# ScalarE's instruction order written out by the program, with the exponentials of masked scores one step behind those taken straight from PSUM

## The chip, the cores and the metric

The kernel runs on one core of one Trainium2 chip. Its time is the device time of one execution, in microseconds (us). The kernel before takes 4256.9 us (the median of 3 executions, 4254.99 to 4259.61). The profile below is of one more execution, with a span of 4253.7 us. TensorE's granted clock was 0.98 of full speed in it.

In what follows PE is TensorE (its matmuls), PEld TensorE's weight loads, ACT ScalarE, DVE VectorE, POOL GpSimd and SP the engine that issues most DMAs. SBUF is the on-chip memory for operands, PSUM the one into which TensorE writes.

## What is computed

Four layers of a graph network run over x, 16 sequences of 1024 nodes with 128 features, with one 1024 x 1024 adjacency matrix for all of them. Three layers are attention layers of 8 heads (16 features a head), each followed by an output projection, a layer norm, a feed-forward part of width 256 and a second layer norm. The fourth is a graph attention layer whose scores are sums of two node values. Cut to what matters here, an attention layer is:

```python
scores = jnp.einsum('bnhd,bmhd->bhnm', Q, K) / jnp.sqrt(16.)
scores = jnp.where(mask, -jnp.inf, scores)          # mask: adj == 0
attn = jax.nn.softmax(scores, axis=-1)
attn_out = jnp.einsum('bhnm,bmhd->bnhd', attn, V).reshape(B, N, OUT_DIM)
x = layer_norm(x + attn_out @ Wo + bo)
x = layer_norm(x + relu(x @ W1 + b1) @ W2 + b2)
```

## The kernel before

**Blocks and steps.** A block is one sequence b in one attention layer l. There are 48 of them, in an order that takes four sequences through three layers side by side. A block has 32 steps: 2 groups g of four heads, 2 halves qh of 512 queries, 8 tiles kt of 128 keys. So there are 1536 steps, numbered n in the main loop (from L703).

**What one step does.** `score_step` (L387) takes an SBUF tile e for the four heads and works on two pairs of heads, pp = 0 and 1. For each pair TensorE writes scores for two heads into a PSUM slot of 128 x 1024 (L395). What then turns scores into masked exponentials goes one of two ways:

- pp = 0 with kt in 0, 1, 3, 4, 6: ScalarE takes the exponential straight out of PSUM (L402), and GpSimd multiplies it by a mask of zeros and ones (L403). There are 960 of these. I call the exponential **direct**.
- pp = 1, and pp = 0 too with kt in 2, 5, 7 (`BOTH_ON_DVE`): VectorE adds a mask of 0 and -57344 while it copies the scores out of PSUM (L405), and ScalarE takes the exponential in place in SBUF (L406). There are 2112 of these. I call this exponential **masked**.

A PSUM slot is free again when L402 or L405 has read it. There are three slots (`slot`, L121), and a step takes two. The fourth layer's edge scores (L569, read by L572) take slots of the same three.

**Four steps later** `av_step` (L409) multiplies e by V on TensorE and adds up in one PSUM bank (L412). The delay is `AHEAD = 4`. There are six e tiles. After the eight tiles kt of a half, `finish` (L415) has VectorE transpose the sums (L423) and take reciprocals (L425), and GpSimd scale them (L426, into A).

**Pieces.** All other work (projections, output projection, feed-forward, the fourth layer) is cut into pieces, and a step takes at most one (`piece`, L642), from chains with due times. A piece writes one PSUM bank, of which there is one only (`bank`, L125). So the next piece's matmuls wait until the bank has been copied out, by ScalarE (L263, L265, L359, L366, L468, L533, L534, L548) or VectorE (L303, L360, L537, L587). For Q and K both do: ScalarE copies a rounded part (hi, L359), then VectorE the remainder (lo, L360).

**Who sets the order.** A scheduler in the compiler decides at build time in which order each engine's instructions stand, from priorities and its own idea of durations; the order does not change while the kernel runs. `soon()` (L251) gives the copies out of the pieces' bank a higher priority. The loop stands inside `tc.manual_schedule` (L704) for TensorE: there instructions stay as the program writes them, score, av, piece, step after step. In the kernel before, this holds for TensorE alone. ScalarE, VectorE and GpSimd are ordered by the scheduler. [...]

In this order of ScalarE the masked exponentials of step n stand, as a rule, before the direct one of step n+1.

## Time and profile before

| engine | busy us | share of the span |
| --- | --- | --- |
| PE (matmuls) | 3892.9 | 92% |
| POOL | 3451.4 | 81% |
| ACT | 3417.3 | 80% |
| DVE | 3404.9 | 80% |
| PEld (weight loads) | 1575.2 | 37% |

The columns come from the first part of the profile page. "Busy" is the time in which at least one instruction of the engine was running. Ends of matmuls are modelled, so a busy TensorE is not TensorE at its peak. DMA is small: the queues moved 232.23 MB, 55 GB/s on average.

A row of the groups of instructions reads: line, engine, operation, tile written <- tiles read, shapes, count | busy us, mean ns of one | idle time of the engine just before them, and which instruction ended most of that idle time. A row of the waits reads: who waited <- for whom: us in total, times, longest. A row of the timeline reads: start, duration, engine, line, operation, tiles, count of merged instructions, and in brackets the idle time before it and what ended it. PEld rows wait while earlier matmuls still run, so a wait shown there is only partly lost time; a wait shown at PE is time without a matmul.

### The profile page before, as it was taken

How to read it: one execution, taken by the hardware profiler on the slowest of the kernel's cores; microseconds unless marked ns; L12 is line 12 of the kernel's file. 1: busy time of each engine (PE TensorE's matmuls, PEld its weight loads, DVE VectorE, ACT ScalarE, POOL GpSimd, SP SyncE). 2: the span in 40 equal slices, each digit the busy share in tenths (PEclk: the TensorE clock that was granted, in tenths of full speed). 3: DMA queues.
4: the chain of work that ended last, by engine and by line, in shares of the span. 5: the costliest groups of instructions: out<-in, count | busy, mean ns of one | idle time of the engine just before them, and what ended most of it. 6: DMA issues, size and time to landing. Idle time of an engine off the chain costs nothing.

```text
span 4253.7 us, 93788 instructions
## 1 busy us (share of the span) xinstructions
PE 3892.9 (92%) x37589; PEld 1575.2 (37%) x37589; DVE 3404.9 (80%) x5324; ACT 3417.3 (80%) x3961; POOL 3451.4 (81%) x3010
## 2 busy tenths in 40 slices
PE   7999999999999999999999899999999999999986
PEld 2333333344443333334444333333344433333435
DVE  6888888877777888887777888887877788888784
ACT  7999999876778898987676898997876789998770
POOL 4788888876779888888777988888877798888785
PEclk9999999999999999999999999999999999999997
DMA  5221222121211221221112212221211212212100
GB/s 147 65 61 50 52 61 61 48 63 44 51 51 48 61 61 44 57 61 51 51 44 59 59 48 55 61 61 41 56 48 49 66 41 61 60 47 55 44 24 17
DMA packets 126235, 232.23 MB, mean 55 GB/s; under 512 B 36704, under 2 KB 75616, under 8 KB 125792
## 3 DMA queue, kind: packets, MB, share of 16 engines
q1 hardware_dynamic: 122896, 225.14, 21.0%
q8 instruction: 299, 4.90, 0.5%
q10 hardware_dynamic: 2896, 1.01, 0.1%
q14 instruction: 144, 1.18, 0.1%
HBM read 15.54 MB, written 8.39 MB: 6 GB/s over the span
## 4 chain that ended last, share of the span: by engine, by line
PE 37%; DVE 26%; ACT 23%; issue 7%; POOL 5%; DMA 1%; SPq 1%; DVEq 0%; ACTq 0%; POOLq 0%
DVE e L405 16%; ACT e L406 13%; PE t L271 11%; PE acc L412 10%; PE s L395 9%; ACT e L402 6%; PE t L581 6%; DVE st L296 2%; POOL e L403 2%; DVE tt L423 1%; DVE e L572 1%; DVE x L303 1%; PE t L260 1%; ACT xT L265 1%; DVE lo L360 1%
## 5 line engine op out<-in xcount | busy, mean ns | idle before, releaser
L405 DVE TENSOR_TENSOR e<-s,mask_add 128x1024 f32<-128x1024 f32 x2112 | 2499.4, 1212 | 441.2 <-PE s L395 351.5
L406 ACT ACTIVATE e<-e 128x1024 f32<-128x1024 f32 x2112 | 2200.2, 1060 | 408.2 <-DVE e L405 392.1
L403 POOL TENSOR_TENSOR e<-e,mask 128x1024 f32<-128x1024 f32 x960 | 2054.0, 2151 | 426.1 <-ACT e L402 410.5
L412 PE MATMUL acc<-e,v 128*17 128x512 f32 x12288 | 1635.4, 604 | 56.5 <-DVE tt L423 29.8
L395 PE MATMUL s<-Wq,Wk 64*128 64x512 f32 x6144 | 1225.7, 462 | 137.9 <-ACT e L402 67.9
L402 ACT ACTIVATE e<-s 128x1024 f32<-128x1024 f32 x960 | 980.4, 1021 | 115.0 <-PE s L395 58.4
L395 PEld LDWEIGHTS s<-Wq,Wk 64*128 64x128 f32 x6144 | 505.8, 185 | 1118.5 <-issue 371.5
L412 PEld LDWEIGHTS acc<-e,v 128*17 128x17 f32 x12288 | 207.2, 95 | 558.2 <-issue 445.6
L315 POOL TENSOR_SCALAR x<-x,mv 128x128 f32<-128x128 f32 x896 | 391.4, 452 | 24.1
L319 POOL TENSOR_TENSOR x<-x,ln_g 128x1024 f32<-128x1024 f32 (+1 forms) x97 | 229.4, 2365 | 107.8 <-PE t L260 101.9
L581 PEld LDWEIGHTS t<-hd,e 128*128 128x128 f32 x2048 | 255.2, 205 | 63.7 <-issue 32.5
L581 PE MATMUL t<-hd,e 128*128 128x129 f32 x2048 | 267.2, 292 | 8.3 <-DVE x L587 3.5
L313 POOL TENSOR_TENSOR mv<-mv,half_neg 128x4 f32<-128x4 f32 x224 | 232.4, 1037 | 14.7
L271 PE MATMUL t<-x1T,W 128*32 128x512 f32 x1536 | 206.2, 609 | 18.0 <-ACT hT L468 8.6
L303 DVE TENSOR_TENSOR x<-t,x 128x512 f32<-128x512 f32 x192 | 131.8, 687 | 100.1 <-PE t L271 99.4
L296 DVE BATCH_NORM_STATS2 st<-x 128x6 f32<-128x128 f32 x896 | 196.7, 279 | 2.8
L271 PEld LDWEIGHTS t<-W,hT 128*32 128x32 f32 x6144 | 172.0, 111 | 70.6 <-issue 32.9
L271 PE MATMUL t<-W,hT 128*32 128x128 f32 x6144 | 187.1, 274 | 9.1 <-DVE x L303 5.2
L260 PE MATMUL t<-identf,x 128*128 128x128 f32 x896 | 151.5, 290 | 34.7 <-ACT xT L265 7.8
L260 PEld LDWEIGHTS t<-identf,x 128*128 128x128 f32 x896 | 95.9, 142 | 229.2 <-issue 48.0
L311 POOL TENSOR_SCALAR mv<-mv 128x4 f32<-128x4 f32 x224 | 53.0, 237 | 145.1 <-DVE mv L298 108.4
L468 ACT ACTIVATE hT<-t,b 128x512 f32<-128x512 f32 x192 | 132.3, 689 | 45.6 <-PE t L271 42.6
(83 smaller groups left out, 2509.7 us busy)
## 6 DMA issues: line engine op xcount, KB each, us to landing
Wk<-hi SPq DMA_DIRECT2D x384, 128.0 KB
Wk<-lo SPq DMA_DIRECT2D x384, 128.0 KB
Wq<-hi SPq DMA_DIRECT2D x384, 128.0 KB
Wq<-lo SPq DMA_DIRECT2D x384, 128.0 KB
x<-in_x_dram SPq DMA_DIRECT2D x16, 512.0 KB
out_dram<-x SPq DMA_DIRECT2D x31, 256.0 KB
ai<-in_adj_dram SPq DMA_DIRECT2D x8, 512.0 KB
g_rows<-parts SPq DMA_DIRECT2D x124, 4.0 KB
```

Source lines behind the costliest of these rows:

```text
L260: nc.tensor.transpose(ps[:, t * P:(t + 1) * P], src[:, 4 * h + t, :], identf)
L271: nc.tensor.matmul(dst[j:j + SLOT, :], lhsT[:, j:j + SLOT], rhs, start=start, stop=stop)
L296: nc.vector.bn_stats(st[:, t, :], z[:, t, :])
L313: nc.gpsimd.tensor_tensor(v, v, half_neg[:, ts], OP.pow)
L315: nc.gpsimd.tensor_scalar(z[:, t, :], z[:, t, :], mv[:, t, 0:1], mv[:, t, 1:2], op0=OP.add, op1=OP.mult)
L395: nc.tensor.matmul(ps[:, r * 512:(r + 1) * 512], k[64 * r:64 * r + 64, kt * P:(kt + 1) * P], q[64 * r:64 * r + 64, q0:q0 + 512], start=Tru ...
L402: nc.scalar.activation(ev, psv, AF.Exp, scale=HD ** -0.5)
L403: nc.gpsimd.tensor_mul(ev, ev, m)
L405: nc.vector.tensor_add(ev, psv, m)
L406: nc.scalar.activation(ev, ev, AF.Exp, scale=HD ** -0.5)
L412: nc.tensor.matmul(acc[j * SLOT:j * SLOT + HD + 1, :], v_bufs[m % 2][:, kt, 2 * j + g, :], e[:, j, :], start=first, stop=last)
L581: nc.tensor.matmul(ps[:, i * (D + 1):(i + 1) * (D + 1)], e[:, t, i * P:(i + 1) * P], s["hd"][t // 4][:, t % 4, :], start=(t == 0), stop=(t ...
```

## The change

The masked exponentials are no longer issued where the add is. `score_step` puts them into a list, and a new function `exponentials` issues them in the program's order. ScalarE joins TensorE inside `manual_schedule`, so it keeps that order. For an entry of step s the number in the list is 2s + pp, plus 1 where the step has a direct exponential. At the end of step s everything below 2s + 1 goes out. So the first masked pair of a step with both pairs on VectorE still goes out in its own step, and every other masked exponential goes out one step later, behind that step's direct one. A copy out of the pieces' bank stands where its piece stands, at the end of its step; the priority that `soon()` gives no longer moves it on ScalarE. The purpose is that ScalarE need not stand before an add that VectorE hasn't finished, with direct exponentials and copies queued behind it. No arithmetic is added or removed.

```diff
             else:
                 nc.vector.tensor_add(ev, psv, m)
-                nc.scalar.activation(ev, ev, AF.Exp, scale=HD ** -0.5)
+                masked.append((2 * step_no[0] + pp + (kt not in BOTH_ON_DVE), ev))
+        step_no[0] += 1
+        exponentials()
         return e
+
+    masked, step_no = [], [0]
+
+    def exponentials(n=None):
+
+        while masked and (n is not None or masked[0][0] < 2 * step_no[0] - 1):
+            _, ev = masked.pop(0)
+            nc.scalar.activation(ev, ev, AF.Exp, scale=HD ** -0.5)
...
-    with tc.manual_schedule(engines={mybir.EngineType.PE}):
+    with tc.manual_schedule(engines={mybir.EngineType.PE, mybir.EngineType.Activation}):
...
                 n += 1
+        exponentials(0)
         for n in range(n, n + 2 * AHEAD):
```

## The prediction

> **What bounds the kernel now.** I read the busy times and slices of the page first, then the groups, then who waited for whom, then the timeline at two places.

> ```profile
> PE   7999999999999999999999899999999999999986
> ...
> DVE  6888888877777888887777888887877788888784
> ACT  7999999876778898987676898997876789998770
> POOL 4788888876779888888777988888877798888785
> ...
> L405 DVE TENSOR_TENSOR e<-s,mask_add 128x1024 f32<-128x1024 f32 x2112 | 2499.4, 1212 | 441.2 <-PE s L395 351.5
> L406 ACT ACTIVATE e<-e 128x1024 f32<-128x1024 f32 x2112 | 2200.2, 1060 | 408.2 <-DVE e L405 392.1
> L403 POOL TENSOR_TENSOR e<-e,mask 128x1024 f32<-128x1024 f32 x960 | 2054.0, 2151 | 426.1 <-ACT e L402 410.5
> ...
> L402 ACT ACTIVATE e<-s 128x1024 f32<-128x1024 f32 x960 | 980.4, 1021 | 115.0 <-PE s L395 58.4
> ```

> No engine is the bound alone. TensorE is at 9 tenths almost everywhere, ScalarE with it in the first six slices (before the fourth layer's work starts) and below it later. ScalarE stands 392.1 us before masked exponentials (L406) whose add (L405) isn't done: 9.2% of the span, half of its idle time. The windows part the kernel by that:

> ```profile
> 60.00:700.00 640.00, 597.17 (x5839) 208.07 (x5837) 541.08 (x778) 582.90 (x651) 542.17 (x444) 1.00 0.25 61
> ...
> 1060.00:2080.00 1020.00, 944.84 (x9112) 380.52 (x9106) 825.69 (x1288) 830.97 (x965) 838.51 (x726) 0.98 0.21 53
> ```

> The columns after the length are PE, PEld, DVE, ACT, POOL: ScalarE is 91% busy in the early window (582.90 of 640) and 81% in the later one. Early, ScalarE's own work leaves little room. Who waits for ScalarE:

> ```profile
> PEld s L395 <- ACT e L402: 237.2, 313, 1.5
> ...
> PEld t L271 <- ACT hT L468: 97.4, 162, 1.5
> ...
> PE s L395 <- ACT e L402: 67.9, 138, 0.9
> ```

> TensorE waits for slots that a direct exponential (L402) holds: 67.9 us with no matmul running, 237.2 us if one counts the weight loads' waits. The next lines are ScalarE's timeline where a copy is stuck:

> ```profile
> 2001.82 0.57 ACT L366 COPY v<-t 128x512 f32<-128x512 f32 x1
> 2002.92 2.19 ACT L406 ACTIVATE e<-e 128x1024 f32<-128x1024 f32 x2 [0.53 <-DVE e L405]
> 2005.02 0.57 ACT L366 COPY v<-t 128x512 f32<-128x512 f32 x1
> ```

> ScalarE stands 0.53 us for an add, runs two masked exponentials, and only then the copy of v for which the next piece waits. TensorE's timeline has that piece (L529) at 2005.64, after 0.34 us of idle.

> [...] the copy at 2005.02 waits behind exponentials that have nothing to do with it. [...]

> **The change, part by part.** No operation is added. I compared the two programs' instruction lists: TensorE's order is the same to the instruction; ScalarE's, VectorE's and GpSimd's differ.

> *Direct exponentials.* 682 of 960 have one masked exponential fewer ahead of them, 47 one more. Each is 1.06 us (1060 ns). The wait to be won is between 67.9 (PE) and 237.2 (PEld); I take the middle, 150 us, since weight loads wait in part under running matmuls. 71% (682/960) is 107 us. Where ScalarE is busy without a gap, one exponential fewer ahead now is one more later, and the wait returns; the early window and the plain steps, without a piece, are like that. I halve: 53 us.

> *Copies out of the pieces' bank.* One or two exponentials fewer stand ahead of 82 of 96 copies of v, 76 of 192 of hT (L468), 33 of 192 with a gain (L265): 191 of 480. For layer 0's input (L263), 21 of 32 have one more. The rows in which TensorE waits for ScalarE's copies of the bank sum to 18.6 + 15.3 = 34 us at PE (L271, L260) and 226.1 + 87.5 = 314 us at PEld (the tile t view of ScalarE). The middle is 174; of it 40% (191/480) is 69 us, and I take 42 us, for the same reason as above. Bounds: 14 (40% of 34) and 125 (40% of 314).

> *The 392.1 us themselves* are no gain but what makes room for it: a masked exponential of the step before, whose add is done, now stands there. In the window 2050 to 2070 TensorE runs the fourth layer's pieces and ScalarE has nothing to do; there the wait costs nothing now and will only carry another name.

> *The wait that the change adds.* A masked exponential now waits behind the next step's direct one, and so for that step's scores. Queued behind it on ScalarE is that step's copy. After it come the sums (L412), four steps later. A step lasts 4253.7/1536 = 2.77 us, so there are some 11 us until e is needed, and the delay is one step: hidden. The six e tiles suffice for the same reason, since the sums' place in TensorE's order is unchanged. Cost 0. During a piece of 5 us (32 matmuls of L581) ScalarE may idle with one exponential undone, 1.06 us that it must make up in the next steps, but the direct one that frees the slot comes before it, so TensorE does not wait for it. Cost 0 to 64 x 1.06 = 68 us; I take 0.

> *VectorE's order.* 62 of 192 subtractions for lo (L360) move behind one more add, 13 move ahead. In 33 of the 62 the next piece comes in the next step, in 29 two steps later, where a step without a piece hides it. The add passed must wait for the next step's scores: from the end of the piece some 0.73 us (scores, 4 matmuls in the timeline), then 1.21 for the add and 0.68 for lo, 2.62 us. The piece could have started after scores and sums, 0.66 + 0.98 = 1.64 us (rows of the chain). So 33 x 0.98 = 32 us; bounds 0 and 33 x 1.21 = 40. I take 30.

> *GpSimd's order.* In 37 of 48 blocks the last scaling (A, L426) moves behind one more multiply of 2.15 us. VectorE's transpose of A (L439) starts 1.79 us after A ends (276.00 + 0.62 to 278.41 in the timeline), and is in VectorE's order ahead of adds. The delay left is 2.15 - 1.79 = 0.36 us if the multiply can start at once. If it starts no earlier than now (276.70, ending 278.86), A ends 279.48 and the transpose is 1.1 us late. 37 x 0.36 = 13, 37 x 1.1 = 41 us of VectorE; half of the lower is on the path, as VectorE is 80% busy: I take 10.

> Sum: 53 + 42 - 30 - 10 = 55 us less: 4256.9 - 55 = 4202 us, 1.3% faster.

> **The rivals.**

> *A, slower.* What the scheduler's priority gave was worth more than what stood in the way. For it: the moved lo and A are at places where VectorE runs without a gap, and in the 60 to 700 window ScalarE is busy at 91%, so hardly any of the wait for L402 can go. Then the gain is the lower bound, 14 + 20 us, the costs the upper ones, 40 + 41, and 21 later copies at 1.06 add 22: 103 - 34 = 69 us at most; half of that, 4291 us. Against it: the counts, 682 to 47 and 191 to 21.

> *B, no change.* TensorE, no longer waiting for L402, waits for the slot of the add instead. For it: PEld waits 338.9 us for L405 on the same matmuls, more than for L402, and VectorE's work is unchanged. Against it: those waits are on VectorE's own order, which hardly moves. 4257 us.

> *C, much faster.* ScalarE's 392.1 us are all filled, and half of them shorten the span, since the later windows are rows of waits in which one engine after the other is late: 196 us, 4061 us. Against it: ScalarE was idle there mostly while TensorE had a long piece, and it will be idle there still.

> **How the numbers follow.** My forecast (20 to 130 us less) has 0.58, C or anything beyond 130 us 0.14, B 0.09, A 0.19. Faster by over 0.2%: 0.72. Within 0.2%: 0.09. Slower: 0.19. The range goes down to 4120 (the forecast's upper bounds together, 237.2 x 0.71 x 0.5 + 125 - 30 - 10 = 169 us, less a part, since they share ScalarE) and up to 4285, close to A's middle. C's far half and A's upper half, 2 in 10, stay outside.

> **What would show it.** The row of masked exponentials should lose most of its 392.1 us behind the adds; the same idle time, less 55 us, then stands before direct exponentials and copies, released by PE. "PE s L395 <- ACT e L402" should fall from 67.9 to about 35 us. "PE t L271 <- DVE lo L360" should rise from 41.1 to about 70, and the transpose of A (L439) should show waits for A, 10.8 us now, of 13 us or more besides. ScalarE's busy time stays at 3417. If masked exponentials still wait over 200 us for adds, the step of one step's delay is wrong; if TensorE's waits for L405 grow by what those for L402 lose, B holds.

## The result, and the profile after

| kernel | median us | range, executions | profiled span |
| --- | --- | --- | --- |
| before | 4255.94 | 4253.97 to 4259.61, 4 | 4253.7 |
| changed | 4236.01 | 4234.81 to 4237.31, 4 | 4233.0 |

The ratio is 0.9952, 95% interval 0.9935 to 0.9969: 20 us or 0.5% faster. The direction was forecast and the time lies in the range of 4120 to 4285, but the gain is 20 us where 55 were forecast.

The slices of the page of the changed kernel:

```profile
PE   7999999999988999999989999999998899999986
...
DVE  6888888877768888888777888888877788888874
ACT  7899999976768999987766899997876689999760
POOL 5888888977769888888766988888886698888785
```

Nothing stands out: each engine is where it was, within a tenth. ScalarE's busy time, which was to stay at 3417 us, is 3396.3; its idle time is 836.7 us (836.4 before). The groups of the same page show where idle time went (masked exponentials are now L417, since lines above 410 moved by ten):

```profile
L405 DVE TENSOR_TENSOR e<-s,mask_add 128x1024 f32<-128x1024 f32 x2112 | 2501.3, 1212 | 427.0 <-PE s L395 307.1
L417 ACT ACTIVATE e<-e 128x1024 f32<-128x1024 f32 x2112 | 2196.3, 1063 | 387.4 <-DVE e L405 369.5
L403 POOL TENSOR_TENSOR e<-e,mask 128x1024 f32<-128x1024 f32 x960 | 2049.4, 2152 | 473.9 <-ACT e L402 469.7
...
L402 ACT ACTIVATE e<-s 128x1024 f32<-128x1024 f32 x960 | 983.8, 1025 | 272.3 <-PE s L395 169.8
```

The masked exponentials' wait for adds, 392.1 us before, is still 369.5. It falls from 446 waits to 378, but those left are longer. I sorted the idle time before masked exponentials by kind, in ScalarE's instruction list. Before: 242.2 us stood at the first masked exponential of a step with two adds, 127.9 at that of a step with one add, 30.9 at the second of a step with two. After: 294.6, 77.7 and 8.6. The change doesn't delay the first kind, and that kind had most of the wait from the start.

The two stretches, early and late (length, then busy time of PE, PEld, DVE, ACT, POOL):

```profile
60.00:700.00 640.00, 601.15 (x5931) 212.15 (x5927) 548.48 (x784) 586.98 (x662) 550.54 (x449) 1.00 0.24 61
1060.00:2080.00 1020.00, 942.69 (x9132) 381.77 (x9136) 829.54 (x1290) 826.84 (x960) 840.67 (x735) 0.98 0.21 53
```

In the early one each engine is some 0.7% to 1.5% busier than before: the same work packed closer. In the late one TensorE and ScalarE are a little less busy in the same time than before. Seen in these two stretches the gain is early; the table of blocks below shows that it isn't so. The waits of the changed kernel:

```profile
PEld s L395 <- DVE e L405: 432.4, 623, 1.9
...
ACT e L402 <- PE s L395: 169.8, 111, 5.7
...
PEld s L395 <- ACT e L402: 109.8, 186, 1.5
...
PEld t L271 <- ACT hT L478: 70.6, 162, 1.1
...
PE s L395 <- DVE e L405: 37.6, 59, 1.7
...
PE s L395 <- ACT e L402: 30.9, 97, 0.6
```

TensorE's wait for direct exponentials fell from 67.9 to 30.9 us, and that of its weight loads from 237.2 to 109.8. But the same weight loads now wait 432.4 us for adds (338.9 before): of the 127 us won, 93 only changed their name. Direct exponentials themselves now wait for scores, 169.8 us against 58.4. The place shown before, a copy of v stuck behind masked exponentials, is now this (timeline of ScalarE):

```profile
1979.39 1.06 ACT L417 ACTIVATE e<-e 128x1024 f32<-128x1024 f32 x1
1980.64 1.06 ACT L417 ACTIVATE e<-e 128x1024 f32<-128x1024 f32 x1 [0.19 <-DVE e L405]
1981.60 0.57 ACT L366 COPY v<-t 128x512 f32<-128x512 f32 x1
```

The copy starts 0.25 us after its piece ends (1.38 us before: the piece ended at 2003.64 there and at 1981.35 here), since of its own step's masked exponentials one is ahead of it and not two (1037 stand ahead of it in all, 1038 before). The next piece (L539) starts at 1982.93 with no idle time of TensorE before it.

**Where the 20 us come from.** The first score matmul of every 32nd step marks the start of a block. From these starts I worked out the 48 block durations of each profile. I number blocks 0 to 47. A plain block is one beside which no work of the fourth layer lies.

| blocks | before, us | changed | difference |
| --- | --- | --- | --- |
| start and block 0 | 108.9 | 105.2 | -3.7 |
| 27 plain blocks (77.1 to 76.1 each, mostly) | 2089.3 | 2062.6 | -26.7 |
| 10, 11, 22, 23, 34, 35, 46 (fourth layer begins) | 646.6 | 631.6 | -15.0 |
| 12, 15, 24, 27, 36, 39 | 580.5 | 574.8 | -5.7 |
| 13 | 109.2 | 109.1 | -0.1 |
| 14, 25, 26, 37, 38 | 508.0 | 537.5 | **+29.5** |
| 47, with the end | 211.1 | 212.1 | +1.0 |

The change gains 50 us over most of the kernel, and loses 29.5 in five blocks of layer 0, in which edges and aggregates of the four sequences before are done. Plain blocks gain about 1 us each early and late alike; the late stretch above holds block 14, which is 5.6 us longer. This table, and not any total of waits, is what showed where to look. Blocks 26 and 25 (in this order) in the windows view, first of the kernel before, then of the changed one (columns as above, then the granted clock):

```profile
2247.10:2345.40 98.30, 92.55 (x884) 42.39 (x880) 79.56 (x135) 69.78 (x79) 71.19 (x64) 0.98 0.23 56
2140.50:2247.10 106.60, 96.07 (x893) 45.83 (x889) 80.10 (x139) 71.59 (x89) 77.44 (x71) 0.95 0.19 51
```

```profile
2227.70:2331.80 104.10, 95.15 (x884) 43.99 (x880) 79.40 (x135) 69.06 (x78) 70.64 (x64) 0.95 0.20 52
2114.90:2227.70 112.80, 99.29 (x893) 46.23 (x889) 80.64 (x139) 71.39 (x89) 79.85 (x71) 0.91 0.19 48
```

The same matmuls (884 and 893) take 2.6 and 3.2 us more of busy time at a lower granted clock (0.98 to 0.95, 0.95 to 0.91), and TensorE is idle 3.2 and 3.0 us more. Over the five blocks TensorE's busy time rises from 469.8 to 483.9, so 14.1 of the 29.5 us are longer busy time of the same matmuls, where the clock is lower, and 15.4 are idle time.

The idle time, at one place of block 26. Timeline of the kernel before:

```profile
2292.48 1.95 PE L271 MATMUL t<-xT,Wq 128*32 128x512 f32 x8
2292.84 2.36 DVE L405 TENSOR_TENSOR e<-s,mask_add 128x1024 f32<-128x1024 f32 x2 [1.35 <-PE acc L412]
...
2294.47 0.59 ACT L359 CAST hi<-t 128x512 fp32r<-128x512 f32 x1 [3.78 <-PE t L271]
2294.96 2.00 ACT L406 ACTIVATE e<-e 128x1024 f32<-128x1024 f32 x2
...
2295.11 0.68 DVE L360 TENSOR_TENSOR lo<-t,hi 128x512 fp32r<-128x512 f32 x1
2296.00 3.84 PE L581 MATMUL t<-hd,e 128*128 128x129 f32 x32
```

and of the changed one:

```profile
2275.48 1.04 PE L271 MATMUL t<-xT,Wq 128*32 128x512 f32 x8
2275.80 2.36 DVE L405 TENSOR_TENSOR e<-s,mask_add 128x1024 f32<-128x1024 f32 x2 [0.55 <-PE acc L422]
...
2277.12 1.06 ACT L417 ACTIVATE e<-e 128x1024 f32<-128x1024 f32 x1 [2.66 <-DVE e L405]
...
2278.09 0.57 ACT L359 CAST hi<-t 128x512 fp32r<-128x512 f32 x1
2278.70 1.23 DVE L405 TENSOR_TENSOR e<-s,mask_add 128x1024 f32<-128x1024 f32 x1 [0.54 <-PE acc L422]
...
2279.84 0.68 DVE L360 TENSOR_TENSOR lo<-t,hi 128x512 fp32r<-128x512 f32 x1
2280.67 5.20 PE L591 MATMUL t<-hd,e 128*128 128x129 f32 x32 [2.11 <-DVE lo L360]
```

Before, the rounded copy hi runs 0.04 us after its piece ends, ahead of the masked exponentials, then lo follows it, and the next piece starts at once. After, a first masked exponential stands ahead of hi. Its add came late, since it waited for sums to free an e tile (2 of the 6 tiles hold edges here). So hi starts 1.57 us after its piece. On VectorE the scheduler has put lo behind one more add as well, and that add comes first. TensorE is idle 2.11 us. Then the next piece, the same 32 matmuls, takes 5.20 us instead of 3.84: the granted clock is 0.72 from 2280 to 2286, where it was 1.00 from 2296 to 2300 in the kernel before.

The two pictures differ in one thing more: the piece at 2292.48 of the kernel before itself took 1.95 us where the changed kernel took 1.04. Nearly all of it lies in a stretch, 2290.95 to 2294.36, in which the granted clock is 0.50 (it is 1.00 beside the changed kernel's piece, 2275.48 to 2276.52). So the loss at this place is less than 2.11 + 1.36 us. From the scores behind the previous aggregate to those behind this one (L395 at 2283.80 and 2299.78 before, 2267.57 and 2285.80 changed) it is 2.25 us.

In each of the five blocks an aggregate waits like this for lo: 2.10, 2.71, 2.11, 2.71 and 2.10 us in blocks 14, 25, 26, 37 and 38, where it waited 0 or 0.24 before. That makes some 11 of the 15.4 us of idle time. Block 13 has such a wait too (2.71 us) and is no longer than before; it has three windows of 3.4 us at half clock, where it had five (the last section tells of these windows).

### The profile page after: what moved, and what is told of

Read it like the earlier page. It is cut to its first block, busy times and chain, and to the rows that moved or that the text cites. A ratio compares the mean times of both kernels' runs of the same rounds, so it can differ in the third digit from the quotient of the medians.

```text
span 4233.0 us, 93837 instructions
## 1 busy us (share of the span) xinstructions
PE 3878.9 (92%) x37589; PEld 1582.0 (37%) x37589; DVE 3405.0 (80%) x5324; ACT 3396.3 (80%) x3961; POOL 3449.9 (82%) x3010
## 4 chain that ended last, share of the span: by engine, by line
PE 48%; DVE 22%; ACT 11%; POOL 9%; issue 9%; SPq 1%; DMA 1%; DVEq 0%; ACTq 0%; POOLq 0%
PE acc L422 15%; PE t L271 12%; PE s L395 11%; DVE e L405 11%; PE t L591 6%; POOL e L403 5%; ACT e L417 5%; ACT e L402 4%; DVE st L296 2%; PE t L260 2%; DVE e L582 2%; DVE lo L360 2%; DVE x L303 1%; POOL x L315 1%; DVE tt L433 1%
## 5 line engine op out<-in xcount | busy, mean ns | idle before, releaser
L405 DVE TENSOR_TENSOR e<-s,mask_add 128x1024 f32<-128x1024 f32 x2112 | 2501.3, 1212 | 427.0 <-PE s L395 307.1
L417 ACT ACTIVATE e<-e 128x1024 f32<-128x1024 f32 x2112 | 2196.3, 1063 | 387.4 <-DVE e L405 369.5
L403 POOL TENSOR_TENSOR e<-e,mask 128x1024 f32<-128x1024 f32 x960 | 2049.4, 2152 | 473.9 <-ACT e L402 469.7
L395 PE MATMUL s<-Wq,Wk 64*128 64x512 f32 x6144 | 1227.4, 462 | 114.4 <-DVE e L405 37.6
L402 ACT ACTIVATE e<-s 128x1024 f32<-128x1024 f32 x960 | 983.8, 1025 | 272.3 <-PE s L395 169.8
L395 PEld LDWEIGHTS s<-Wq,Wk 64*128 64x128 f32 x6144 | 504.8, 186 | 1087.1 <-DVE e L405 432.4
L315 POOL TENSOR_SCALAR x<-x,mv 128x128 f32<-128x128 f32 x896 | 392.1, 453 | 24.1
L591 PE MATMUL t<-hd,e 128*128 128x129 f32 x2048 | 267.4, 292 | 22.3 <-DVE lo L360 17.0
L591 PEld LDWEIGHTS t<-hd,e 128*128 128x128 f32 x2048 | 255.6, 206 | 81.9 <-issue 53.7
L313 POOL TENSOR_TENSOR mv<-mv,half_neg 128x4 f32<-128x4 f32 x224 | 232.3, 1037 | 18.3
L271 PE MATMUL t<-x1T,W 128*32 128x512 f32 x1536 | 200.8, 594 | 3.4 <-DVE x L597 1.0
L271 PEld LDWEIGHTS t<-W,hT 128*32 128x32 f32 x6144 | 171.2, 110 | 70.5 <-issue 32.6
L271 PE MATMUL t<-W,hT 128*32 128x128 f32 x6144 | 186.3, 273 | 7.9 <-DVE x L303 3.7
L260 PE MATMUL t<-identf,x 128*128 128x128 f32 x896 | 149.6, 291 | 42.7 <-DVE lo L360 21.6
L260 PEld LDWEIGHTS t<-identf,x 128*128 128x128 f32 x896 | 96.3, 143 | 236.5 <-issue 89.5
L594 DVE RECIPROCAL col<-t 128x2 f32<-128x2 f32 x64 | 10.9, 170 | 185.7 <-PE t L591 185.7
```

The lines of the kernel that those rows point to most:

```text
L260: nc.tensor.transpose(ps[:, t * P:(t + 1) * P], src[:, 4 * h + t, :], identf)
L271: nc.tensor.matmul(dst[j:j + SLOT, :], lhsT[:, j:j + SLOT], rhs, start=start, stop=stop)
L313: nc.gpsimd.tensor_tensor(v, v, half_neg[:, ts], OP.pow)
L315: nc.gpsimd.tensor_scalar(z[:, t, :], z[:, t, :], mv[:, t, 0:1], mv[:, t, 1:2], op0=OP.add, op1=OP.mult)
L395: nc.tensor.matmul(ps[:, r * 512:(r + 1) * 512], k[64 * r:64 * r + 64, kt * P:(kt + 1) * P], q[64 * r:64 * r + 64, q0:q0 + 512], start=Tru ...
L402: nc.scalar.activation(ev, psv, AF.Exp, scale=HD ** -0.5)
```

## The experiments

Times are given as ratios to the kernel before, run on the same chip in the same rounds. "The changed kernel" is the one above, 0.9952.

**1. The two halves of the edit alone.** The changed kernel, with each masked exponential issued right behind its add:

```diff
-                masked.append((2 * step_no[0] + pp + (kt not in BOTH_ON_DVE), ev))
+                nc.scalar.activation(ev, ev, AF.Exp, scale=HD ** -0.5)
```

> The other part of the change alone: ScalarE in the program's order, but each masked exponential where it was, right behind its add, so before its step's copy and before the next step's direct one. Theory 1 (the step's delay is what pays, a ScalarE that stands before adds costs): slower than before, 4270 to 4320 us, with waits for adds of 500 us or more. Theory 2 (what little is won comes from fixing the order as such): 4230 to 4245 us, like the change.

Measured: 4651.08 us, ratio 1.0945 (1.093 to 1.096), much slower than either theory had it.

```profile
L406 ACT ACTIVATE e<-e 128x1024 f32<-128x1024 f32 x2112 | 2218.3, 1058 | 906.8 <-DVE e L405 884.4
```

The wait for adds more than doubles, and plain blocks take 86 to 87 us. And the other half, the delayed list with ScalarE left to the scheduler:

```diff
-    with tc.manual_schedule(engines={mybir.EngineType.PE, mybir.EngineType.Activation}):
+    with tc.manual_schedule(engines={mybir.EngineType.PE}):
```

> One part of the change alone: the masked exponentials are issued one step later in the program's text, but ScalarE stays with the scheduler (only TensorE's order is fixed), so copies out of the pieces' bank stand where they stood before, except that 31 of 192 with a gain (L265) stand one exponential later. lo is one add later in 56 places and A one multiply later in 82, about as in the change. If the direct exponentials' place is what pays: as fast as the change, 4230 to 4240 us. If the earlier copies pay (my term of 42 us): no more than 10 us of gain is left, 4246 to 4258 us.

Measured: 4253.19 us, ratio 1.0004 (0.9996 to 1.0012); waits for adds 406.0 us; plain blocks 77.4 us. (The profile behind the waits and block times has a span of 4242.1 us, some 9 us less than the median execution.) So neither half gains anything: without the scheduler the delay is needed not to lose 9%, and with the scheduler the place in the program hardly matters. In the five blocks, however, this kernel takes 507.6 us, like the one before (508.0). The loss there belongs to the order being fixed.

By the expectation this points to the copies as what pays: TensorE's wait for direct exponentials is most of the way down (39.3 us, 139.8 for weight loads), its wait for ScalarE's copies of the bank is not (39.9 us; 33.9 before, 14.8 changed), and nothing is gained. But its waits for lo and A are those of the changed kernel (75.7 and 17.2 us), so a gain of the direct exponentials may be there and be eaten by them. The run doesn't part the two.

**2. The forecast's costs: lo and A.** In the changed kernel, the add after a lo is queued behind it (the scheduler of VectorE is told so):

```diff
-                    nc.vector.tensor_sub(lo[:, c], ps, hi[:, c].bitcast(F32))
+                    ahead['add'] = nc.vector.tensor_sub(lo[:, c], ps, hi[:, c].bitcast(F32))
...
-                nc.vector.tensor_add(ev, psv, m)
+                with behind('add'):
+                    nc.vector.tensor_add(ev, psv, m)
...
+    def behind(what):
+        ins = ahead.pop(what, None)
+        return tc.issue_after(getattr(ins, "ins", ins)) if ins is not None and started else nullcontext()
```

> The changed kernel, with one thing put back: each subtraction for lo (L360) is again queued on VectorE ahead of the next step's add, as it was before the change (no lo stands later than in the kernel before, 24 stand one add earlier). ScalarE's order is that of the changed kernel. Theory 1 (the change did gain what the forecast says on ScalarE, and the scheduler's moves on VectorE ate a good part of it, lo 30 us of it): about 4206 us against 4236 for the change, and TensorE's waits for lo, 77.7 us in the changed kernel (35.9 + 21.6 + 17.0 + 3.2), fall to 55 or less. Theory 2 (the gain on ScalarE was over-estimated, since TensorE now waits for the slot of the add instead): lo's place is worth little, 4230 to 4236 us, and where the wait for lo goes, one for adds (L405) comes.

Measured: 4242.23 us, ratio 0.9978 (0.9969 to 0.9986); span 4234.5. This is slower than both theories had it; TensorE's waits for lo fall to 70 us and not to 55. The same for GpSimd, the next multiply queued behind the scaling of A:

```diff
-                nc.gpsimd.tensor_mul(ev, ev, m)
+                with behind('mul'):
+                    nc.gpsimd.tensor_mul(ev, ev, m)
...
-            nc.gpsimd.tensor_mul(state["A"][:, qh, :, g, :], tt[:, :, :HD],
+            ahead['mul'] = nc.gpsimd.tensor_mul(state["A"][:, qh, :, g, :], tt[:, :, :HD],
```

> The changed kernel, with GpSimd's last scaling of a block (A) queued again ahead of the multiply that had slipped in front of it. Theory 1 (side moves ate the gain): 10 us less than the change, 4226 us, and VectorE's transpose of A waits 0 to 3 us for A in place of 18.0. Theory 2 (VectorE's delay there lies off the path): 4233 to 4238 us, with the same fall of that wait.

Measured: 4234.71 us, ratio 0.9961 (0.9947 to 0.9974); span 4230.9. The time is theory 2's, but the transpose of A still waits 10.5 us for A, as in the kernel before. Each edit takes 0.3 us off a plain block (76.1 to 75.8), so the two costs are real there, some 8 us each over 27 blocks. But put ahead everywhere, lo costs elsewhere what it gains: blocks 11, 23 and 35 go from 81.8 to about 85 us, and in all VectorE stands 64.5 us before lo for hi (12.3 in the changed kernel), with adds queued behind it. In the five blocks it gives 12.6 of the 29.5 us back (524.9). With A ahead, 5.9 us are lost in blocks 10, 11, 22, 23, 34, 35 and 46, and 3.6 in block 13. Neither alone is the way to the missing gain.

**3. How late the masked exponentials should be.** Here the first masked exponential of a two-add step goes behind the piece of its step and that piece's copy, instead of ahead:

```diff
-                masked.append((2 * step_no[0] + pp + (kt not in BOTH_ON_DVE), ev))
+                masked.append((2 * step_no[0] + pp, ev))
...
-        while masked and (n is not None or masked[0][0] < 2 * step_no[0] - 1):
+        while masked and masked[0][0] < 2 * step_no[0] - 2 + below:
...
                 piece()
+                exponentials(1)
```

> The changed kernel with the first masked exponential of a step with two adds issued behind the copy of that step's piece, in place of ahead of it; all else as in the change. In the changed kernel 294.6 of the 381 us that ScalarE stands before masked exponentials stand before just these. Theory 1 (such a wait is lost where a copy stands behind it): 20 to 40 us less than the change, 4196 to 4216 us, and TensorE's waits for ScalarE's copies (15 us at PE, 261 us at PEld in the changed kernel) fall by half. Theory 2 (ScalarE has room there, TensorE or VectorE being the bound in those steps): within 10 us of the change, 4226 to 4246 us.

Measured: 4269.35 us, ratio 1.0042 (1.0028 to 1.0055), slower than both theories had it. ScalarE's waits:

```profile
ACT e L417 <- DVE e L405: 150.1, 231, 3.0
ACT e L402 <- PE s L395: 136.7, 109, 5.1
ACT hi L359 <- PE t L271: 120.9, 97, 3.8
```

The wait for adds falls by 219 us against the changed kernel, and the kernel is slower. The rows show why this can be: the masked exponentials now stand behind copies that wait for their pieces (120.9 us for hi). In plain blocks 76.7 us instead of 76.1. Next, all masked exponentials one full step late:

```diff
-                masked.append((2 * step_no[0] + pp + (kt not in BOTH_ON_DVE), ev))
+                masked.append((2 * step_no[0] + 1, ev))
```

> The changed kernel with the first masked exponential of a step with two adds issued one step later too, like all others (three of them in a row in the step after). In the changed kernel these 576 hold 294.6 us of the waits for adds. Theory 1 (waits for adds are lost time): the waits fall under 120 us and the kernel gains a good part of the difference, 30 to 80 us less than the change, 4155 to 4206 us. Theory 2 (such a wait only takes the place of one that ScalarE would have anyway, before scores or pieces): the waits fall as much, those for TensorE rise by as much, and the time is within 15 us of the change, 4221 to 4251 us.

Measured: 4254.93 us, ratio 1.0007 (0.9999 to 1.0015), a little over what theory 2 said.

```profile
ACT e L402 <- PE s L395: 244.2, 157, 6.5
...
ACT hi L359 <- PE t L271: 101.8, 67, 5.4
...
ACT e L417 <- DVE e L405: 47.4, 54, 2.8
```

Of the 392.1 us that the prediction began with, 345 are gone, and the time is that of the kernel before. So this wait, as a total, doesn't tell the time. By blocks the equal times hide two things: plain blocks take 76.3 us, nearly as in the changed kernel (76.1), though their waits for adds fell from 102.8 to 17.2 us; and against the kernel before, the 21 us that they gain are lost again, 12.5 of them in the five blocks, 5.3 in 12, 15, 24, 27, 36 and 39 and 4.3 in the last. Then two steps late:

```diff
-        while masked and (n is not None or masked[0][0] < 2 * step_no[0] - 1):
+        while masked and (n is not None or masked[0][0] < 2 * step_no[0] - 3):
```

> All masked exponentials two steps later than their adds, so that hardly any can stand before an add. It shows how much there is to win by this at all. Theory 1 (392 us of waits were worth a good part of their length): waits for adds under 30 us, and 4130 to 4200 us. Theory 2 (they are the slack of an engine that is 80% busy and has to wait for TensorE): waits for adds under 30 us, ScalarE's idle time as a whole unchanged, some 830 us, and 4221 to 4260 us, with more of TensorE's waits for multiplies and exponentials before the sums, since two steps less are left until e is needed.

Measured: 4200.21 us, ratio 0.988 (0.9865 to 0.9895).

```profile
PE 44%; POOL 20%; DVE 19%; ACT 11%; issue 5%; DMA 1%; SPq 1%; DVEq 0%; ACTq 0%; POOLq 0%
...
L417 ACT ACTIVATE e<-e 128x1024 f32<-128x1024 f32 x2112 | 2134.1, 1058 | 1.9 <-DVE e L405 1.8
```

The wait for adds is gone, TensorE waits 1.0 us for direct exponentials with no matmul running, and plain blocks take 75.2 us. The time is at the edge of theory 1; ScalarE's idle time, 822.0 us, is what theory 2 said: direct exponentials now wait 261.5 us for scores (58.4 before). GpSimd is now on the chain of work that ended last (20%; 5% before, 9% changed). The sums come four steps after the scores, so two steps of delay still fit. Why this second step of delay gains 1.1 us a plain block, where the edit before it gained nothing there, I can't say; this stays open.

A last one on the delay: the prediction costed at 0 the masked exponential left undone while TensorE has a piece of 32 matmuls (bound 68 us). Here what is left in the list is issued in the step of such a piece, right behind the piece's own instructions:

```diff
             if now[0] >= chain["due"] + chain["queue"][0][0] and take(chain):
+                if long_piece:
+                    long_piece.clear()
+                    exponentials(0)
                 return
```

> The changed kernel, but when the step's piece is one of the 64 long ones (32 matmuls of L591, over 4 us), all masked exponentials that are left are issued in that step, ahead of the next direct one, so that ScalarE has them to run during the piece. My forecast put the cost of leaving them undone at 0, with 68 us as its upper end. Theory 1 (0 was right, the direct exponential comes first anyway): within 8 us of the change, 4228 to 4244 us. Theory 2 (the deferral costs ScalarE work that it can't make up): 20 to 60 us less than the change, 4176 to 4216 us, and its waits for scores (169.8 us in the changed kernel) fall by 40 us or more.

Measured: 4238.22 us, ratio 0.9969 (0.9956 to 0.9981), a little over the changed kernel, with intervals that overlap. Theory 1 holds: there is no cost to be won back.

**4. The blocks that lost.** The changed kernel, but with ScalarE's order by the scheduler in the five blocks and block 13:

```diff
-    with tc.manual_schedule(engines={mybir.EngineType.PE, mybir.EngineType.Activation}):
-        for m, (b, l) in enumerate(blocks):
+    for m, (b, l) in enumerate(blocks):
+        with tc.manual_schedule(engines={mybir.EngineType.PE} if m in (13, 14, 25, 26, 37, 38) else PE_ACT):
```

> The changed kernel, but in six of the 48 blocks (layer 0, lanes 1 and 2, of passes 1 to 3: the ones in which the fourth layer's edges and aggregates of the pass before lie) ScalarE's order is again the scheduler's. Theory (order in those blocks costs what the rest gains): the five blocks that the change made longer, 112.8, 112.9, 103.8, 104.1 and 103.8 us, return to 106.6, 106.6, 98.2, 98.3 and 98.3, some 29 us in all, and the other blocks stay (76.1 us a plain one): about 4236 - 29 = 4207 us, ratio 0.988 to 0.9895. Rival (the blocks are longer because of what the blocks before them hand over, not because of the order in them): 4230 to 4240 us.

Measured: 4214.07 us, ratio 0.9914 (0.9902 to 0.9927), span 4207.8. Blocks 26 and 25 in the windows view:

```profile
2217.30:2315.60 98.30, 92.57 (x886) 42.60 (x882) 79.61 (x135) 69.84 (x79) 71.23 (x64) 0.98 0.22 56
2109.80:2217.30 107.50, 95.68 (x893) 45.90 (x889) 79.92 (x139) 71.83 (x89) 78.70 (x71) 0.95 0.20 50
```

Length, busy time and clock are those of the kernel before, within 1 us and 0.01. The five blocks take 509.7 us: 27.8 of the 29.5 us are back. The aggregate's late wait for lo is gone in all of them. The span is 25.2 us shorter than that of the changed kernel (4207 was expected); by the ratios the gain is 0.4%, some 16 us, less than the 0.988 to 0.9895 expected. So ScalarE's order within these blocks made the loss, idle time and clock both (VectorE's order there followed it: lo is back at its old places too). Which part of the order? The changed kernel with the first masked exponential of a two-add step behind the piece, as in the first kernel of part 3, in these six blocks only:

```diff
-                masked.append((2 * step_no[0] + pp + (kt not in BOTH_ON_DVE), ev))
+                masked.append((4 * step_no[0] + (2 if pp else step_no[0] // 32 in SIX), ev))
...
                 piece()
+                exponentials(1)
```

> The changed kernel, but in the same six blocks the first masked exponential of a two-add step is issued behind that step's piece and its copy; everything else as it is. Theory (copy hi stands behind a masked exponential whose add is late): TensorE's late pieces there come back in part; lo still stands behind the next add on VectorE, as the order of VectorE isn't touched. With all blocks treated so the five lasted 109.3, 109.3, 101.4, 101.8 and 101.3 us: 3.5 + 3.6 + 2.4 + 2.3 + 2.5 = 14 us less, about 4222 us, ratio 0.992 to 0.9935. Rival (hi isn't the first cause, lo behind the add is): no more than 4 us less, 4232 to 4240 us.

Measured: 4219.33 us, ratio 0.9931 (0.9918 to 0.9944), span 4217.8. At the place shown in block 26 this kernel has:

```profile
2271.53 0.59 ACT L359 CAST hi<-t 128x512 fp32r<-128x512 f32 x1 [3.42 <-PE t L271]
2272.01 1.06 ACT L419 ACTIVATE e<-e 128x1024 f32<-128x1024 f32 x1
...
2272.16 0.68 DVE L360 TENSOR_TENSOR lo<-t,hi 128x512 fp32r<-128x512 f32 x1
...
2273.29 3.85 PE L593 MATMUL t<-hd,e 128*128 128x129 f32 x32
```

hi is ahead of the masked exponential again, lo follows at once, and the next piece takes 3.85 us (3.84 in the kernel before) and not 5.20. The waits of such aggregates for lo fall from 11.7 to 2.5 us over the five blocks. These take 520.4 us, so 17.1 of the 29.5 are back, as expected. Three limits of this. The expectation took VectorE's order as untouched, but it wasn't: with hi ahead the scheduler put lo back ahead of the add at all six places (56 of 192 lo stand one add later than in the kernel before, 62 in the changed kernel). So the run undoes hi and lo together. The edit also moves every first masked exponential of these blocks behind its piece, not only the one ahead of the late hi. And the ratio's interval overlaps a little with that of the changed kernel, so the 17.1 us are read from one profile of each. With lo queued ahead of the next add as well (part 2's edit over the whole kernel):

> The same with the next add queued behind lo, so that both of the copies that the piece's bank waits for are ahead of what stood in their way. Theory (the two in a row make the loss, neither alone): the five blocks get near 106.6 and 98.3 us, some 25 us less than the changed kernel, 4207 to 4215 us, ratio 0.988 to 0.991. Rival (hi alone is the cause): as without the change to lo, 4222 us; rival (lo queued ahead holds up the adds, as when it was done alone, which took 4242 us): over 4230 us.

Measured: 4231.27 us, ratio 0.9959 (0.9946 to 0.9973). The five blocks are unchanged, 520.2 us, so lo is not what is left there. It was already ahead there. Since lo ahead alone, with hi still late, had given 12.6 us back (part 2), most of the 17.1 us seem to come through lo: by these figures hi late by itself costs some 5 us (524.9 against 520.2), and lo, which moved behind the add together with hi, the rest. The two steps (six blocks' order, lo) don't add up, because lo ahead costs 13.4 us in blocks 10, 11, 22, 23, 34 and 35 (534.4 to 547.8). The remaining 10 us or so of the five blocks come back with the scheduler's whole order. Most of them are TensorE's busy time (477.7 us, 469.3 with the scheduler's order, at 15 and 9 windows of half clock); I didn't trace them to one instruction.

Last, two steps of delay and the scheduler's order in the six blocks, together:

> All masked exponentials two steps late (4200 us when alone), and in the same six blocks ScalarE's order by the scheduler. Theory: the six blocks, 112.9, 99.5, 111.2, 101.2, 112.5 and 100.1 us with two steps, go to about 106.4 and 98.4 with the add's delay gone: 6.5 + 1 + 5 + 3 + 6 + 2 = 23 us less, about 4178 us, ratio 0.981 to 0.984. Rival (a scheduler's block between two blocks with a two-step delay pays at its edges, with up to four masked exponentials handed over): within 5 us of 4200 us, or more.

Measured: 4184.16 us, ratio 0.9839 (0.9826 to 0.9852), the best of all: 1.6% faster than before. The six blocks take 617.1 us (637.3 with two steps alone, 617.3 before) and plain blocks 75.1. It is 6 us short of what was expected, since blocks that I had left out of the sum got longer: 5.4 us in 10, 11, 22, 23, 34, 35 and 3.7 in the last.

## Why the prediction was right and wrong

The step that failed first is a term left at nothing: the copies hi were not in the sum. Six of them came to stand behind a masked exponential whose add was late, and the six lo after them behind one more add. ScalarE's order in five of these blocks cost 29.5 us. With the scheduler's order there, 27.8 come back; with first masked exponentials behind the pieces, and hi and lo so back at their places, 17.1. By the ratios of all executions the first of these kernels gains 36 us, so some 16 of the 35 us that were missing lay there (25 by the profiled spans). The rest is size: the direct exponentials, forecast at 53, won less. The terms against the waits that the prediction named, before and after:

| term | forecast | measured | how |
| --- | --- | --- | --- |
| direct exponentials | +53 | +33 | waits for L402 less what those for L405 gained: 37.0 - 4.8 at PE, 127.4 - 93.5 at PEld, the middle |
| copies out of the bank | +42 | +36 | 33.9 to 14.8 at PE, 313.6 to 261.2 at PEld, the middle |
| lo | -30 | -23 | TensorE's waits for lo at PE, 55.3 to 78.4 (13.7 of it at the aggregates behind the late hi) |
| A | -10 | -7 | transposes' wait for A, 10.8 to 18.0 |
| clock | not there | -14 | TensorE's busy time in the five blocks, 469.8 to 483.9 |
| sum | +55 | +25 | the spans differ by 20.7 |

This is bookkeeping in the forecast's own way, not proof of each term, and that it comes near 20.7 is in part luck: TensorE's busy time outside the five blocks also fell, by 28.1 us (3423.1 to 3395.0), and no row has that.

**The term left out.** I counted how far copies of v, hT, gains and the input moved on ScalarE, and said nothing of hi: 172 of its 192 copies keep their place, 14 come earlier, and 6 come one exponential later. I passed over the 6. They are one in each of blocks 13, 14, 25, 26, 37 and 38. The lo behind each is among the 62 that I did count, there at 0.98 us or at nothing. A count weighs all places alike; these lie where add, e tile, bank and lo are all tight, and one exponential there made TensorE wait 2.11 us at the place shown.

**The clock.** The prediction had none in it: a late piece was costed at its delay. Nearly as much came on top, as longer busy time where the clock is at half (14.1 of 29.5 us), which is told below.

**Direct exponentials, mis-sized.** The fall of "PE s L395 <- ACT e L402" was forecast to 35 us, and was to 30.9. But three quarters of what the weight loads won (93 of 127 us) they now wait for adds. This is rival B, which I gave 0.09 and which holds for this term in good part, though not for the whole: the plain blocks did get 1 us shorter. Where the forecast expected the won time to return, in the early window, it didn't: blocks 2 to 8 got 1 us shorter each, as much as plain blocks later.

**One step of delay, wrong.** "Should lose most of its 392.1 us": it lost 22.6. By the prediction's own rule (over 200 us left) this step failed. The change delays only the second masked exponential of a two-add step and the one of a one-add step, and those had 159 of the 401 us of my count; I had taken the wait as evenly spread. What that did to the time isn't settled: with the wait nearly gone (47.4 us) the kernel takes 4255 us, with all of it gone (1.8) 4200. "The 392.1 us themselves are no gain" fits the first; in the second, too, ScalarE idles as long as before (822.0 and 836.4 us), only elsewhere.

**lo, right in size by luck.** The waits of TensorE for lo, before:

```profile
PE t L271 <- DVE lo L360: 41.1, 47, 1.5
...
PE t L260 <- DVE lo L360: 6.0, 6, 1.1
...
PE t L581 <- DVE lo L360: 3.3, 6, 0.9
```

and changed:

```profile
PE t L271 <- DVE lo L360: 35.9, 43, 1.5
...
PE t L260 <- DVE lo L360: 21.6, 30, 1.0
...
PE t L591 <- DVE lo L360: 17.0, 12, 2.1
```

The row named, at L271, was to rise to 70 and fell. The rise at the aggregates (L581, now L591) goes with the late hi: it is 3.3 again with the scheduler's order in the six blocks. The rise at L260 goes with A: it is 6.5 with A put ahead (part 2). So the 23 us are not the sum that was forecast, 33 pieces late by some 1 us each: 13.7 of them lie at the places with the late hi, of which the forecast knew nothing.

**A**: its own row is 18.0 us in 32 waits against 10.8 in 5 before, just over half of the rise forecast, and the waits at L260 belong to it too. **The delayed masked exponential** cost 0 in long pieces, as taken. That a copy on ScalarE waits behind what stands ahead of it shows in the gain and in the loss: at the places shown the copy of v starts 0.25 us after its piece, with one masked exponential of its step ahead of it, where it was 1.38 us with two, and hi starts 1.57 us after its piece, behind an exponential that it doesn't need.

Rival A, slower, named the kind of cause that did lose time: that the scheduler's order of copies was worth more than what stood in the way. It holds in five blocks of 48. Of its own instances the moved lo has a part in that, where it moved with hi; for A no run shows one.

## To carry to other kernels

Work out the gain and loss by stage before believing a total: here 50 us won and 29.5 lost hid in 20. When an order is fixed by the program, look up every copy that frees a buffer with a single holder and see what stands ahead of it, above all where the buffers are shared with another job; a count of instructions that keep their place doesn't show it. And the delay of software pipelining is worth trying at one more and one less, and per stage: one step late for most gave 0.5%, one step late for all nothing, two steps late 1.2%, and two steps with the scheduler's order where that was better 1.6%.

## What was not expected of the hardware

| kernel | slow windows, in all | in blocks 14, 25, 26, 37, 38 | these blocks, us |
| --- | --- | --- | --- |
| before | 50 | 9 | 508.0 |
| changed | 60 | 21 | 537.5 |
| delayed list, ScalarE scheduled | 43 | 7 | 507.6 |
| scheduled in the six blocks | 50 | 9 | 509.7 |
| first ones behind the piece in the six blocks | 56 | 15 | 520.4 |
| two steps | 57 | 14 | 524.4 |
| two steps, scheduled in the six blocks | 57 | 9 | 509.6 |

(The kernel with masked exponentials right behind their adds has 121.) Twelve more slow windows in the five blocks are 20.5 us of lost clock; TensorE's busy time there rose by 14.1. At the place shown in block 26, an idle time of 2.11 us was followed by a piece that took 1.36 us longer. As an estimate from these figures, an idle time of 2 us in this kernel can have cost up to 3.7: itself, and the 1.71 us of a slow window. No experiment took the clock alone, by keeping TensorE busy over an idle place, so the part of it is read from the records and not tested by an edit.
